# Convolution transforms by sums and differences of mirrored steps, with each block's odd token tiles reversed up to the MLP

## The chip, the core and the metric

The kernel runs on one core of a Trainium2 chip. The metric is the device time of one execution in microseconds, lower is better. The core has a matrix engine (TensorE, PE in the profile; its weight loads are PEld), a vector engine (VectorE, DVE), an activation engine (ScalarE, ACT), a general engine (GpSimd, POOL) and a queue that issues most of the loads (SyncE, SP).

## The reference, cut to what matters

One transformer layer over 8 blocks of 512 tokens by 256 features. The part that the change touches is a causal convolution of each feature along the 512 tokens (steps) of a block, written with Fourier transforms, between two scale-and-shift steps:

```python
x = layernorm(x_text) ; scale_in, shift_in = split(c_t @ W_film_in + b_film_in)
x = x * (1 + gate * scale_in) + gate * shift_in
# s4d: causal convolution along the steps, by Fourier transforms of length 2 L
Kf = rfft(K, n=2 * L); xf = rfft(x, n=2 * L, axis=1)
y  = irfft(xf * Kf, n=2 * L, axis=1)[:, :L] + x * D_skip      # here L = 512 steps
y  = y * (1 + gate * scale_out) + gate * shift_out
xt = x_text + y
h  = gelu(layernorm(xt) @ W1 + b1) @ W2 + b2
xt = layernorm(xt + h)
```

Ahead of it stands an attention of the tokens over 1024 context rows (4 heads, the 32 largest scores of each row are kept), whose result `c_t` makes the scales and shifts. Behind it stands a mixture of experts: a shared expert for every token, and one of 8 routed experts, chosen per token.

## The kernel before, in words

**Tiles.** A block's 512 tokens are four tiles of 128 partitions by 256 features. `xm` (input of the convolution), `xr` (its output and then the running sum), `s.xt` (the normalised input) hold these four tiles side by side. The convolution of 512 steps is done on two halves of 256 steps each (in the kernel `L = T // 2 = 256`), with transforms of length 512 that share tables; the second half also gets the first half's share by a second kernel spectrum. Tile t is (half b, part c) with t = 2 b + c, and a product of 512 columns takes part c of both halves at once.

**Transforms.** `ftab` holds cosine and sine tables for 256 frequencies by 256 steps, in 128x128 pieces. `spectrum(src, f, r, name)` makes frequency group f (128 of them) of part r (real, imaginary) with a product over each of the two step groups c. So `mixed` (one call per block) issues for f and r in 0, 1 two products each, 8 of 128x128 by 512 columns, into PSUM tiles `pxf`. VectorE multiplies them with the kernel's spectrum `kf` (tiles `t2`, `t3`, shown as `t`), GpSimd sums into `yf`. The way back is again 8 products, 4 for each step group c, into `py`; ScalarE copies each to `xr`, then two of the four tiles are multiplied and shifted by `film` (its product is `pfo`; `pfi` is the one ahead of the convolution).

**Around it.** `prepare` loads a block (`xt`, `cx`), normalises, transposes with `ident`, and makes queries and keys; it runs one to two blocks ahead. `attention` makes scores (`pS`), finds the 32 largest (`mn`, `hi`, `top`), and weighs the context rows (`e`, `acc`, `pa`, `pu`). `after_mix` normalises (`hh`), transposes (`transposed`, `hT`), runs the MLP (`pm` into `ga`, `am` into the running accumulators `acc`), adds to `xr`, normalises twice more, and runs router and shared expert (`pg`, `p`, `ae`). `routed` runs blocks of one expert's 128 tokens (`pg`, `pu`, `pyr`). Small constant tables are made in `setup`, beside the attention of block 0; there the spectrum of the convolution's own kernel is made from `ktime` into `pf`, then `kf`.

**Order.** Nothing runs in program order. Every operation is noted with a cost by the class `Plan` (`note`, `time`), and `order` lays them out at build time as a list schedule: on each engine, whenever it is free, the ready operation with the lowest number. Attention and `prepare` have their numbers lowered by 100 (`LEAD_A`, `LEAD_P`), the scores raised by 300 (`LEAD_S`). Buffers of one tag are granted in the order in which the tiles were made. `together` interleaves the notes of three streams: attention of block b, everything behind attention of block b - 1 (`behind`), `prepare` of b + 1. On the chip each engine, and SP, then takes its instructions strictly in the planned order. Since all of them are issued from `o.fn()` in `issue`, nearly every operation bears line 323 in the profile; tiles tell them apart.

**Buffers.** General PSUM tiles (`bank`) share 4 banks, tag "mm"; film products and accumulators (`bank2`) have 2, tag "ac". Weights come in 5 buffers of 128x1024, tag "w" (`wpool`): in setup first the time tables `qq`, then `film_in`, `film_out`, then `w1` and `w2` of block 0.

Of the kernel before, what the change touches and what calls it, by code (L numbers as in the profile page):

```python
# [12 lines left out]
F32 = mybir.dt.float32  # L13
# [5 lines left out]
ALU = mybir.AluOpType  # L19
# [3 lines left out]
P = 128  # L23
# [320 lines left out]
def tile_kernel(ctx: ExitStack, tc: tile.TileContext, a: dict, out: bass.AP):  # L344
# [13 lines left out]

    L = T // 2
# [36 lines left out]
    def bank(name, pool=ps_mm, tag="mm"):  # L396
        return pool.tile([P, 512], F32, tag=tag, name=name)
# [4 lines left out]
    def accs(name):  # L402
# [14 lines left out]
                     base=0, channel_multiplier=-1)  # L417
    plan.noting = True
# [12 lines left out]
    def prepare(b, s):  # L431
# [89 lines left out]

    ftab = const.tile([P, 3, NL, L], F32, name="ftab")

# [34 lines left out]
    def row(v, n):  # L558
        return v.rearrange("(o d) -> o d", o=1).broadcast_to([n, v.shape[0]])
# [21 lines left out]
    def transposed(src, tag, name, g=None, b=None):  # L581

        t_ = pr.tile([P, ND, T], F32, tag=tag, name=name)
        for c in range(ND):
            p_ = bank(f"{name}_p{c}")
            for t in range(NT):
                TE.transpose(p_[:, t * P : (t + 1) * P], src[:, t, c * P : (c + 1) * P], ident)
# [6 lines left out]
    def spectrum(src, f, r, name):  # L594

        p_ = bank(name)
        blocks = src.rearrange("p (b c) d -> p c b d", b=2)
        for c in range(NL):
            TE.matmul(p_, ftab[:, r, c, f * P : (f + 1) * P], blocks[:, c],
                      start=(c == 0), stop=(c == NL - 1))  # L600
        return p_.rearrange("p (b d) -> p b d", b=2)


    def setup():
# [248 lines left out]
        V.memset(cf[0:1, 0:1], 1.0 / NFFT)  # L853
        for f in range(NL):
            for r in range(2):
                p3 = spectrum(ktime, f, r, f"pf{f}_{r}")
# [4 lines left out]
                V.scalar_tensor_tensor(k1, k0, alt, k1, ALU.mult, ALU.add)  # L861
            for k in kf:
                V.tensor_copy(k[:, f, 2, :], k[:, f, 0, :])
# [193 lines left out]
    def mixed(b, s):  # L1057
# [9 lines left out]

        yf = pr.tile([P, NL, 2, 2, D], F32, tag="yf", name=f"yf{b}")
        for f in range(NL):
            re, im = (spectrum(xm, f, r, f"pxf{b}_{f}_{r}") for r in range(2))  # L1070
# [12 lines left out]
            yield  # L1083
        xr = s.xr = pr.tile([P, NT, D], F32, tag="xr", name=f"xr{b}")
        for c in range(NL):
            p_ = bank(f"py{b}_{c}")
            steps = [(f, r) for f in range(NL) for r in range(2)]
            for i, (f, r) in enumerate(steps):
                TE.matmul(p_, ftab[:, 2 * r, f, c * P : (c + 1) * P], yf[:, f, r].rearrange("p b d -> p (b d)"),
                          start=(i == 0), stop=(i == len(steps) - 1))  # L1090
            S.copy(xr.rearrange("p (b c) d -> p c b d", b=2)[:, c], p_.rearrange("p (b d) -> p b d", b=2))
            for t in (c, NL + c):
                p_ = film(1, s, t, f"pfo{b}_{t}")
                V.tensor_mul(xr[:, t, :], xr[:, t, :], p_[:, :D])
                V.tensor_add(xr[:, t, :], xr[:, t, :], p_[:, D:])
                GP.tensor_add(xr[:, t, :], xr[:, t, :], s.xt[:, t, :])
            yield

    def after_mix(b, s, between=()):
# [28 lines left out]
        for i in range(2):  # L1128
            V.tensor_add(xr[:, 2 * i : 2 * i + 2], xr[:, 2 * i : 2 * i + 2], acc[i])
# [288 lines left out]
    with tc.If(rows_ok < P):  # L1418
# [6 lines left out]
        V.tensor_copy(tmask, pt[:, : B * NT])  # L1425
        for t_ in (cum, pdone):
            GP.memset(t_, 0.0)
# [54 lines left out]
```

## Time and profile before

| | |
|---|---|
| median of 3 runs | 1792.97 us (1792.47 to 1794.63) |
| the profiled execution | 1794.11 us |
| its span, first to last instruction | 1792.3 us |
| instructions | 21191 |
| mean granted TensorE clock | 0.874 of full |
| PE / DVE / ACT / POOL busy | 1513.1 / 1302.1 / 1154.6 / 931.5 us |

A group line reads: line of the program, engine, operation, output and inputs by the program's names, shapes, count; then the time in which at least one of the group ran, the mean length of one in ns; then the idle time of its engine just before them and what ended it. A window line has the stretch in us, its length, the busy time of PE, PEld, DVE, ACT and POOL with the count of instructions, the granted clock (1.00 is full), the share of the DMA engines and GB/s. A wait line says which engine and tile waited for what: us in total, number of times, longest. An fp32 matrix product appears as two MATMUL records, a transpose as one. Neighbouring matmuls overlap in the record, so sums go by the busy time and not by count times mean.

### The profile page before, as it was taken

The numbers are of one execution on the slowest core, as the hardware profiler recorded it, in microseconds if no ns is written. First come the engines' busy times: TensorE is split into PE (matmuls) and PEld (weight loads), VectorE is DVE, ScalarE is ACT, GpSimd is POOL, SyncE is SP. The second block draws the span as 40 slices with busy tenths as digits, with TensorE's granted clock in tenths as the row PEclk, the third lists the DMA queues.
The fourth block names the chain that finished last, engine by engine and source line by source line (L and its number), as shares of the span: only waits on it lengthen the run. The fifth ranks groups of instructions, "written<-read, shape, count | busy, mean of one in ns | idle before, by whom it ended". The sixth has DMA issues, their size and how long they took to land. (4 is left out here: it accounts for less than half of the span.)

```text
span 1792.3 us, 21191 instructions
## 1 busy us (share of the span) xinstructions
PE 1513.1 (84%) x6363; PEld 893.1 (50%) x6363; DVE 1302.1 (73%) x3073; ACT 1154.6 (64%) x2008; POOL 931.5 (52%) x1072
## 2 busy tenths in 40 slices
PE   5365577797998798999889999998999989889885
PEld 2143333344543454465436554654465547547685
DVE  6989977885878697977798889697978987222210
ACT  4778844676747774887578877885788678123121
POOL 5578544445363645465555765474557646233122
PEclk8555677786998799998989999998999989989898
DMA  4000110001200120143103330431033205523794
GB/s 118 0 1 24 33 35 18 12 12 47 70 20 12 47 65 18 36 128 96 54 12 109 91 102 12 135 107 58 12 111 107 66 12 162 179 103 86 228 280 117
DMA packets 101289, 131.68 MB, mean 73 GB/s; under 512 B 9687, under 2 KB 73004, under 8 KB 101166
## 3 DMA queue, kind: packets, MB, share of 16 engines
q1 hardware_dynamic: 93102, 121.05, 21.1%
q0 software_dynamic: 7008, 8.42, 2.6%
q8 instruction: 52, 0.85, 0.2%
q10 hardware_dynamic: 1056, 0.79, 0.1%
q14 instruction: 71, 0.58, 0.1%
HBM read 112.22 MB, written 18.78 MB: 73 GB/s over the span
## 5 line engine op out<-in xcount | busy, mean ns | idle before, releaser
L323 PE MATMUL pS<-kT,qT 32*128 32x512 f32 x512 | 285.6, 742 | 71.2 <-DVE mn L323 61.0
L323 POOL TENSOR_TENSOR acc<-acc,e 128x1024 f32<-128x1024 f32 x96 | 229.0, 2385 | 182.3 <-ACT e L323 179.9
L323 DVE MAX8 top<-mn 128x8 f32<-128x256 f32 (+1 forms) x512 | 276.0, 556 | 11.9
L323 ACT COPY sc<-pS 128x512 f32<-128x512 f32 x256 | 145.6, 584 | 167.1 <-PE pS L323 136.9
L323 DVE SCALAR_TENSOR_TENSOR e<-sc,t,e 128x1024 f32<-128x1024 f32 x128 | 180.3, 1421 | 40.6 <-ACT e L323 40.3
L323 DVE TENSOR_TENSOR mn<-sc,pS 128x512 f32<-128x512 f32 x256 | 165.2, 677 | 35.9 <-PE pS L323 19.9
L323 POOL TENSOR_TENSOR mn<-mn 128x256 int32<-128x256 int32 x128 | 102.4, 800 | 164.4 <-DVE hi L323 163.8
L323 PEld LDWEIGHTS pS<-kT,qT 32*128 32x128 f32 x512 | 75.9, 208 | 203.6 <-DVE mn L323 98.9
L323 ACT ACTIVATE e<-sc,sm 128x1024 f32<-128x1024 f32 x128 | 145.1, 1146 | 16.1 <-POOL acc L323 13.2
L323 ACT ACT_TABLE_LOAD x118 | 151.4, 1283 | 4.0 <-issue 2.0
L323 PE MATMUL pm<-hT,w 128*128 128x512 f32 x256 | 137.9, 677 | 13.6 <-ACT hT L323 13.6
L323 ACT ACTIVATE junk<-sc,sm 128x1024 bf16<-128x1024 f32 x128 | 146.1, 1141 | 1.3
L323 PEld LDWEIGHTS pu<-aT,cx 128*96 128x96 f32 x1024 | 122.2, 168 | 28.6 <-issue 24.1
L323 PE MATMUL pu<-aT,cx 128*96 128x128 f32 x1024 | 135.4, 282 | 0.2 <-ACT aT L323 0.2
L323 PE MATMUL am<-w,ga 128*128 128x256 f32 x512 | 129.1, 398 | 6.1 <-ACT ga L323 6.1
L323 PEld LDWEIGHTS am<-w,ga 128*128 128x128 f32 x512 | 96.9, 196 | 51.4 <-issue 27.6
L323 POOL DMA_INDIRECT out_dram<-yb,to x38 | 61.5, 1620 | 96.7 <-DMA out_dram<-yb,to 46.3
L323 ACT ACTIVATE e<-e,sm 128x1024 f32<-128x1024 f32 x96 | 108.5, 1147 | 1.6 <-DVE sm L323 1.6
L323 POOL TENSOR_TENSOR mn<-mn,hi 128x256 int32<-128x256 int32 x128 | 104.9, 819 | 8.0
L323 DVE TENSOR_TENSOR ger<-sgr,pu 128x512 f32<-128x512 f32 x38 | 26.0, 684 | 108.7 <-PE pu L323 105.9
L323 DVE MATCH_REPLACE8 mn<-top,mn 128x256 f32<-128x256 f32 x256 | 104.6, 409 | 0.0
L323 POOL TENSOR_TENSOR yf<-yf,t 128x512 f32<-128x512 f32 (+1 forms) x80 | 85.2, 1089 | 35.0 <-DVE t L323 33.7
(287 smaller groups left out, 3125.0 us busy)
## 6 DMA issues: line engine op xcount, KB each, us to landing
rt_gate<-in_L_ffn_rt_gate_dram SPq DMA_DIRECT2D x38, 512.0 KB
rt_up<-in_L_ffn_rt_up_dram SPq DMA_DIRECT2D x38, 512.0 KB
rt_down<-in_L_ffn_rt_down_dram SPq DMA_DIRECT2D x38, 512.0 KB
w<-in_L_xattn_W_dram SPq DMA_DIRECT2D x32, 512.0 KB
cx<-in_ctx_dram SPq DMA_DIRECT2D x7, 768.0 KB
xtab<-zt SPq DMA_DIRECT2D x8, 642.5 KB
xb<-xtab SPq DMA_DIRECT2D x38, 128.5 KB
xt<-in_x_dram SPq DMA_DIRECT2D x8, 512.0 KB
```

What stands on the lines that cost most here:

```text
L323: o.fn()
```

## The change

The second part of each half (odd tiles t = 1 and 3, 128 steps) is kept in reverse order of its tokens from `prepare` to the MLP. Step p of an even tile then lies on the same partition as its mirror step L - 1 - p in the odd tile. A cosine or sine table at half-step offset is even or odd under this mirroring, depending on the parity of the frequency. So the frequencies are grouped by parity instead of by halves of the range, and each group's real and imaginary part needs only the sum or only the difference of the two tiles: one product of 128 steps instead of two. Backwards, the four spectra give two results, `pyu` and `pyw`, with two products each, whose sum and difference are the even and odd tiles.

- `prepare` transposes the odd tiles with `anti` (ones on the counter-diagonal) in place of `ident`, then reverses the odd tiles of `s.xt` and of its scale `rs2` by products with `anti` (`pr`) and copies on ScalarE.
- `mixed` makes `df` and the sum in place of `xs` on VectorE, four products, four backwards, one copy, a subtraction and an addition on VectorE; then film for the four tiles.
- `after_mix` transposes `hh`'s odd tiles with `anti`, which puts the MLP's input back in token order. `xr`'s odd tiles are added to the MLP's accumulators by a product with `anti`, and copied out by ScalarE; the even tiles are added by VectorE as before.
- `setup` loads the tables as `ktab` and `htab` (in the "w" buffers) and sorts them into `ftab` and `itab` by three copies on ScalarE. The spectrum of the kernel itself is still made with two products each, with columns picked by parity; `spectrum` is gone.
- The general pass (`attention_masked`, only where a check at the end fails) gets its token mask reversed.

```diff
+    anti = const.tile([P, P], F32, name="anti")
+    GP.memset(anti, 0.0)
+    GP.affine_select(anti, anti, pattern=[[1, P]], compare_op=ALU.not_equal, fill=1.0,
+                     base=-(P - 1), channel_multiplier=1)
+    turn = (ident, anti)
...
-                TE.transpose(p_[:, t * P : (t + 1) * P], s.xt[:, t, c * P : (c + 1) * P], ident)
+                TE.transpose(p_[:, t * P : (t + 1) * P], s.xt[:, t, c * P : (c + 1) * P], turn[t % 2])
             S.copy(xT[:, c, :], p_)
         yield
+        for v, n in ((s.xt, D), (s.rs2.unsqueeze(2), 1)):
+            p_ = bank(f"pr{b}_{n}")[:, : 2 * n].rearrange("p (b d) -> p b d", b=2)
+            x1 = v.rearrange("p (b c) d -> p c b d", c=2)[:, 1]
+            TE.matmul(p_, anti, x1, start=True, stop=True)
+            S.copy(x1, p_)
...
-    ftab = const.tile([P, 3, NL, L], F32, name="ftab")
+    ftab = const.tile([P, 2, 2, P], F32, name="ftab")
+    itab = const.tile([P, 2, 2, P], F32, name="itab")
...
-        for i, r in enumerate((0, 1, 1)):
-            SY.dma_start(ftab[:, i], ft[:, 0, r, :NL, :L])
+        ktab = wpool.tile([P, 1024], F32, tag="w", name="ktab").rearrange("p (r c f) -> p r c f", r=2, c=NL)
+        htab = wpool.tile([P, 1024], F32, tag="w", name="htab")[:, : 2 * L].rearrange("p (r f) -> p r f", r=2)
+        for r in range(2):
+            SY.dma_start(ktab[:, r], ft[:, 0, r, :NL, :L])
+            SY.dma_start(htab[:, r], ft[:, 1, r, 0, :L])
+        S.copy(ftab, htab.rearrange("p r (j g) -> p r g j", g=2))
+        S.copy(itab[:, 0], ktab[:, :, 0].rearrange("p r (n two) -> p two r n", two=2)[:, 1])
+        S.copy(itab[:, 1], htab.rearrange("p r (n two) -> p two r n", two=2)[:, 1])
+        SY.dma_start(ftab[:, 1, 0, 0:1], altc)
+        SY.dma_start(itab[0:1, 0, 1, :], altr)
         for c in range(NL):
-            SY.dma_start(ftab[:, 1, c, 0:1], altc)
-            SY.dma_start(ftab[0:1, 2, 0, c * P : (c + 1) * P], altr)
+            SY.dma_start(ktab[:, 1, c, 0:1], altc)
...
+        xs, xd = (xm.rearrange("p (b c) d -> p c b d", c=2)[:, k] for k in range(2))
+        df = pk.tile([P, 2, D], F32, tag="sg", name=f"df{b}")
+        V.tensor_sub(df, xs, xd)
+        V.tensor_add(xs, xs, xd)
...
-            re, im = (spectrum(xm, f, r, f"pxf{b}_{f}_{r}") for r in range(2))
+            re, im = bank(f"pxf{b}_{f}_0"), bank(f"pxf{b}_{f}_1")
+            for r, p_ in enumerate((re, im)):
+                TE.matmul(p_, ftab[:, r, f], xs if f == r else df, start=True, stop=True)
...
-        for c in range(NL):
-            p_ = bank(f"py{b}_{c}")
-            steps = [(f, r) for f in range(NL) for r in range(2)]
-            for i, (f, r) in enumerate(steps):
-                TE.matmul(p_, ftab[:, 2 * r, f, c * P : (c + 1) * P], yf[:, f, r].rearrange("p b d -> p (b d)"),
-                          start=(i == 0), stop=(i == len(steps) - 1))
-            S.copy(xr.rearrange("p (b c) d -> p c b d", b=2)[:, c], p_.rearrange("p (b d) -> p b d", b=2))
-            for t in (c, NL + c):
...
+        pu, pw = bank(f"pyu{b}"), bank(f"pyw{b}")
+        for p_, k in ((pu, 0), (pw, 1)):
+            for f in range(NL):
+                r = f if k == 0 else 1 - f
+                TE.matmul(p_, itab[:, f, r], yf[:, f, r].rearrange("p b d -> p (b d)"),
+                          start=(f == 0), stop=(f == NL - 1))
+        x0, x1 = (xr.rearrange("p (b c) d -> p c b d", c=2)[:, k] for k in range(2))
+        pw3 = pw.rearrange("p (b d) -> p b d", b=2)
+        S.copy(x0, pu.rearrange("p (b d) -> p b d", b=2))
+        V.tensor_sub(x1, x0, pw3)
+        V.tensor_add(x0, x0, pw3)
+        for t in range(NT):
...
-        hT = transposed(hh, "hT", f"hT{b}", gff, bff)
+        hT = transposed(hh, "hT", f"hT{b}", gff, bff, turn)
...
+            if k == 0:
+                for t in range(1, NT, 2):
+                    TE.matmul(acc[t // 2][:, 1, :], anti, xr[:, t, :], start=False, stop=False,
+                              skip_group_check=True)
...
-            V.tensor_add(xr[:, 2 * i : 2 * i + 2], xr[:, 2 * i : 2 * i + 2], acc[i])
+            V.tensor_add(xr[:, 2 * i], xr[:, 2 * i], acc[i][:, 0])
+            S.copy(xr[:, 2 * i + 1], acc[i][:, 1])
```

More of the change, by code (lines that the diff above doesn't have):

```diff
@@ L579, in normalise, with transposed @@
                          scale=rs[:, t : t + 1])
-    def transposed(src, tag, name, g=None, b=None):
+    def transposed(src, tag, name, g=None, b=None, turn=(ident, ident)):
         t_ = pr.tile([P, ND, T], F32, tag=tag, name=name)
@@ L586, in transposed @@
             for t in range(NT):
-                TE.transpose(p_[:, t * P : (t + 1) * P], src[:, t, c * P : (c + 1) * P], ident)
+                TE.transpose(p_[:, t * P : (t + 1) * P], src[:, t, c * P : (c + 1) * P], turn[t % 2])
             if g is None:
@@ L592, in transposed @@
         return t_
-    def spectrum(src, f, r, name):
-        p_ = bank(name)
-        blocks = src.rearrange("p (b c) d -> p c b d", b=2)
-        for c in range(NL):
-            TE.matmul(p_, ftab[:, r, c, f * P : (f + 1) * P], blocks[:, c],
-                      start=(c == 0), stop=(c == NL - 1))
-        return p_.rearrange("p (b d) -> p b d", b=2)
     def setup():
@@ L853, in setup @@
         V.memset(cf[0:1, 0:1], 1.0 / NFFT)
+        ktab_ = ktab.rearrange("p r c (j g) -> p r c g j", g=2)
+        lags = ktime.rearrange("p (b c) d -> p c b d", b=2)
         for f in range(NL):
             for r in range(2):
-                p3 = spectrum(ktime, f, r, f"pf{f}_{r}")
+                p_ = bank(f"pf{f}_{r}")
+                for c in range(NL):
+                    TE.matmul(p_, ktab_[:, r, c, f], lags[:, c], start=(c == 0), stop=(c == NL - 1))
+                p3 = p_.rearrange("p (b d) -> p b d", b=2)
                 c_ = cf[:, f : f + 1]
@@ L860, in setup @@
                 V.tensor_scalar(k1, p3[:, 1], c_, None, ALU.mult)
-                V.scalar_tensor_tensor(k1, k0, alt, k1, ALU.mult, ALU.add)
+                V.tensor_tensor(k1, k1, k0, ALU.subtract if f else ALU.add)
             for k in kf:
@@ L1065, in mixed @@
             yield
+        xs, xd = (xm.rearrange("p (b c) d -> p c b d", c=2)[:, k] for k in range(2))
+        df = pk.tile([P, 2, D], F32, tag="sg", name=f"df{b}")
+        V.tensor_sub(df, xs, xd)
+        V.tensor_add(xs, xs, xd)
         yf = pr.tile([P, NL, 2, 2, D], F32, tag="yf", name=f"yf{b}")
         for f in range(NL):
-            re, im = (spectrum(xm, f, r, f"pxf{b}_{f}_{r}") for r in range(2))
+            re, im = bank(f"pxf{b}_{f}_0"), bank(f"pxf{b}_{f}_1")
+            for r, p_ in enumerate((re, im)):
+                TE.matmul(p_, ftab[:, r, f], xs if f == r else df, start=True, stop=True)
+            re, im = (p_.rearrange("p (b d) -> p b d", b=2) for p_ in (re, im))
             y = yf[:, f]
@@ L1084, in mixed @@
         xr = s.xr = pr.tile([P, NT, D], F32, tag="xr", name=f"xr{b}")
-        for c in range(NL):
-            p_ = bank(f"py{b}_{c}")
-            steps = [(f, r) for f in range(NL) for r in range(2)]
-            for i, (f, r) in enumerate(steps):
-                TE.matmul(p_, ftab[:, 2 * r, f, c * P : (c + 1) * P], yf[:, f, r].rearrange("p b d -> p (b d)"),
-                          start=(i == 0), stop=(i == len(steps) - 1))
-            S.copy(xr.rearrange("p (b c) d -> p c b d", b=2)[:, c], p_.rearrange("p (b d) -> p b d", b=2))
-            for t in (c, NL + c):
[L1093 to L1097, printed above, removed]
+        pu, pw = bank(f"pyu{b}"), bank(f"pyw{b}")
[10 more added lines that the diff above has]
+        for t in range(NT):
+            p_ = film(1, s, t, f"pfo{b}_{t}")
+            V.tensor_mul(xr[:, t, :], xr[:, t, :], p_[:, :D])
+            V.tensor_add(xr[:, t, :], xr[:, t, :], p_[:, D:])
+            GP.tensor_add(xr[:, t, :], xr[:, t, :], s.xt[:, t, :])
+            if t % 2:
+                yield
     def after_mix(b, s, between=()):
@@ L1425, in tile_kernel @@
         V.tensor_copy(tmask, pt[:, : B * NT])
+        pt = bank("pt_an")
+        TE.matmul(pt[:, : B * NT], anti, tmask, start=True, stop=True)
+        odd = slice(1, B * NT, 2)
+        V.tensor_copy(tmask[:, odd], pt[:, odd])
         for t_ in (cum, pdone):
```

## The prediction

> **What bounds the kernel now.** I read four views in this order: the page's busy shares and slices, one window over the steady stretch, the waits of TensorE in it, and four windows around the convolution.
>
> ```profile
> PE 1513.1 (84%) x6363; PEld 893.1 (50%) x6363; DVE 1302.1 (73%) x3073; ACT 1154.6 (64%) x2008; POOL 931.5 (52%) x1072
> PE   5365577797998798999889999998999989889885
> ...
> DVE  6989977885878697977798889697978987222210
> ...
> PEclk8555677786998799998989999998999989989898
> ```
>
> Three stages show. Up to about 315 us (seven slices) VectorE is nearly full, TensorE half busy at half clock: setup beside block 0's attention. From about 630 to 1530 us TensorE stands at 8 to 9: one block's attention beside the convolution, MLP and experts of the block before. Behind 1530 us the last block runs with VectorE almost empty. The time is mostly made in the middle one:
>
> ```profile
> 630.00:1530.00 900.00, 841.71 (x3440) 491.32 (x3439) 746.32 (x1836) 681.18 (x1174) 519.93 (x624) 0.95 0.25 75
> ```
>
> The columns are length, then PE, PEld, DVE, ACT, POOL busy. TensorE is busy 841.7 of 900 us, VectorE 746.3: 94% against 83%. What TensorE waits for in that window:
>
> ```profile
> PE pc L323 <- DMA cx<-in_ctx_dram: 15.8, 3, 6.0
> PE pyr L323 <- DVE ger L323: 11.0, 7, 3.1
> PE hT_p L323 <- ACT hh L323: 10.2, 5, 3.8
> PE pm L323 <- ACT hT L323: 7.9, 5, 4.6
> PE pS L323 <- ACT sc L323: 4.6, 4, 2.3
> PE pS L323 <- DVE mn L323: 3.8, 6, 1.2
> ```
>
> Its scores (`pS`) wait 3.8 us for VectorE in 900. So in this stage VectorE does not hold TensorE up; TensorE is the nearer bound, with a load (`cx`) and the normalisation chain behind the convolution (`hh`, `hT`) as the gaps. The same around the forward transform of four blocks:
>
> ```profile
> 870.00:890.00 20.00, 20.00 (x57) 8.64 (x55) 18.04 (x34) 10.96 (x20) 13.21 (x9) 1.00 0.00 0
> 1050.00:1070.00 20.00, 20.00 (x55) 8.39 (x54) 16.56 (x32) 14.28 (x22) 15.19 (x13) 1.00 0.26 73
> 1230.00:1260.00 30.00, 30.00 (x74) 12.78 (x73) 22.30 (x47) 15.58 (x29) 14.10 (x13) 0.85 0.00 0
> 1410.00:1440.00 30.00, 29.43 (x87) 13.39 (x87) 28.28 (x63) 15.42 (x26) 20.50 (x21) 1.00 0.00 1
> ```
>
> TensorE is full (99.4 of 100 us), but VectorE has 85.2: little room for what the change puts there.
>
> **The change part by part.** Rows by shape that price it:
>
> ```profile
> L323 PE MATMUL py<-yf,ftab 128*128 128x512 f32 x128 | 58.8, 600 | 0.7 <-POOL yf L323 0.7
> L323 PE MATMUL pxf<-xm,ftab 128*128 128x512 f32 x128 | 58.8, 600 | 0.0
> L323 DVE TENSOR_TENSOR t<-pxf,kf 128x512 f32<-128x512 f32 x32 | 21.2, 680 | 1.4 <-POOL yf L323 1.4
> L323 DVE TENSOR_TENSOR ta<-ta,tk 128x512 f32<-128x512 f32 x8 | 12.9, 1616 | 0.2
> L323 DVE TENSOR_TENSOR tk<-tk,ta 128x512 f32<-128x512 f32 x8 | 9.0, 1126 | 6.2 <-POOL ta L323 6.0
> L323 PE MATMUL am<-w,ga 128*128 128x256 f32 x512 | 129.1, 398 | 6.1 <-ACT ga L323 6.1
> ```
>
> An fp32 product is two records, so 8 products each of `pxf` and `py` per block are 64 products a group, and 58.8/64 = 0.92 us each. By the busy time, not by the mean of 600 ns, since neighbours overlap.
>
> Forward transform: 8 products become 4: -3.67 us of TensorE. Before them VectorE makes a difference and a sum (`df`, `xs`) of 128x512, both inputs in SBUF: 2 x 1.13 to 2 x 1.62 us. [...] They stand between `xm` and the first product, and need all four tiles of it where the first two sufficed before.
>
> Inverse: 8 products become 4: -3.67 us. ScalarE copies once instead of twice (-0.58, `xr<-py` 583 ns), VectorE subtracts and adds from PSUM: 2 x 0.68 = 1.36 us. All four tiles wait for them; before, two tiles went ahead. Both `pyu` and `pyw` hold a PSUM bank for these 1.36 us longer. Other users of these four banks pay at most that in turn; I take nothing, as the removed products free the same banks earlier.
>
> Reversal of odd tiles in `prepare`: transposes with `anti` cost what those with `ident` cost. Added are one product of 512 columns (0.92), one of 2 columns (at most the 0.31 of a `pg<-gate,hdT` product, 19.9/64), and two ScalarE copies (0.585 and about 0.2, as `sm<-t` of 128x2). TensorE +1.2, ScalarE +0.8 us. It runs a block ahead of its reader, so the copies are hidden behind attention; TensorE's 1.2 is not where it is full. Without the cover ScalarE's copies cost 0.8 us a block.
>
> MLP: two products of 256 columns (129.1/256 = 0.50 each): +1.0 us. VectorE adds 2 x 128x256 (0.42) instead of 2 x 128x512 (0.68), -0.5; ScalarE copies the other two tiles, +0.73 (`xbT<-pxb`, 365 ns).
>
> Per block: TensorE -7.35 + 1.2 + 1.0 = -5.1; VectorE 2.7 + 1.36 - 0.5 = +3.6; ScalarE -0.58 + 0.8 + 0.73 = +0.95; GpSimd nothing. Over eight blocks -41, +28, +8 us.
>
> Setup: three table loads of 256 KB become two of 256 and two of 128 KB, four one-element-column loads remain four. So SP issues 8 where it issued 7. The old loads were issued at 17 to 24 us into own memory; `ktab` and `htab` take two of the five `w` buffers and can only load when the time table's `qq` lets go, where SP now issues the first `w1` (191 us) and three more `w` (213 to 226 us). These `w` move two places back; their first reader is at 363 us, so over 100 us cover it, and without the cover it would be two loads of some 4 us. `ktab`'s reader `pf` starts at 238.7 us; between lie the landing, an ACT copy (`itab`), and the small `alt` loads behind that copy on SP. SP's queue there holds the parameter loads that the setup's end waits for. I take +1 us, from 0 to +6 if SP or ScalarE stand in line. Three ScalarE copies (0.6 + 2 x 0.4) are in it, and a memset and a select on GpSimd at the start (0.2 + 0.28 us by `ident`'s) lie before its 6.7 us wait.
>
> Last block (behind 1540 us): attention is gone, the chain is bare. `xm` is complete at 1567.8, `pxf` starts at 1568.4, GpSimd's first sums at 1572.2, the second end at 1583.4, `py` ends at 1586.4. New: sums of 2 x 1.13, then two products instead of four: GpSimd starts about 0.7 later; behind its end 2 products instead of 4 are left (-1.8), then subtract and add (+1.36) and two more tiles of film on VectorE (+1.7). With +1.0 and -0.5 of the MLP I come to about +1 us, from -2 to +3. The expert loads behind 1676 us are not touched.
>
> Blocks 0 to 6, two views. By the whole block of 180 us: TensorE 169 -> 163.9 at the same 93.9% is -5.5 us; VectorE then has 153.8 of 174.5, 88%. By the stage alone: the four windows' VectorE work of 85.2 plus 4 x 4.1 = 101.6 us at 97%, the most it reaches for long, is 104.7 us against 100: +1.2 each, with 1.2 for the reversal in full windows and 0.7 of the MLP +3.1. The truth depends on whether attention's VectorE work is displaced into the later windows of the block, where VectorE has some 10 us free. The missing wait of `pS` for VectorE speaks for the first view; I take -2.5 of the span -5.5 to +3.1.
>
> [...] The row: granted clock 0.59 at 920 to 930 us, where TensorE waited for `hh` and `hT`, and 0.50 through most of the setup. [...] Removed products lengthen such gaps. [...]
>
> Sum: 7 x -2.5 + 1 + 1 = -15.5 us. The profiled execution took 1794.1 us (span 1792.3), 1.1 above the median of 1793.0; so 1793 - 15 = 1778.
>
> **The rivals.**
>
> 1. VectorE becomes the bound of the convolution's stage: 7 x 3.1 + 2 = +24, or about 1812 with some of attention displaced (+19). For it: VectorE at 9.5 to 9.9 us in 10 through much of 880 to 930, 1250 to 1300 and 1400 to 1460 us. Against: 83% over the block. It decides once VectorE has over 97% of the stretch from `pfi` to `pm` while TensorE waits for `df`, `xs` or `hh`.
>
> 2. Everything is gained: -5.1 to -5.5 in each of seven blocks, 1757. Against: the gaps at `cx` (33.8 us in the whole trace) and `hh` are not TensorE's work and remain.
>
> 3. The gain turns into the wait for `cx`. The load of the block after next is issued when the last `pu` of a block has read the buffer, and TensorE stands in order before it, 5 to 6 us at 860 and 1222 us. The order is written by the planner from its costs, so changed costs move such waits; one more or less in each of three blocks is 16 us either way, and with the gain eaten it is no change, 1793.
>
> 4. The whole is not what it says: a failed check at the end would run the general pass over all blocks. The counts it tests don't depend on token order; under 1%.
>
> **How the numbers follow.** The forecast (own range 1766 to 1788) 0.45; rival 1 0.36; rival 2 0.05; rival 3 0.13, of which no change 0.07, slower 0.04 and faster 0.02; rival 4 0.01. Faster 0.52, within 0.2% (3.6 us, about what a measurement can tell apart) 0.07, slower 0.41. The range goes from full gain with one wait less in hand, 1755, to rival 1 without displacement, 1817.
>
> **What would show it.** Right: `pxf` and `py` groups at half their count and about 29 us each; TensorE's busy sum near 1470; blocks of 177 to 178 us between forward transforms; `df` and `xs` of 1.1 to 1.6 us. Wrong: TensorE below 92% in 630 to 1530 us with waits for `df`, `xs`, `x1` or a longer one for `hh`; granted clock lower behind the convolution; `ktab` copies with ScalarE idle before them; more than 15.8 us of wait for `cx`.

## The result, and the profile after

| | before | after |
|---|---|---|
| median of 4 runs each | 1793.72 us (1792.47 to 1794.63) | 1864.76 us (1860.91 to 1867.97) |
| ratio | 1 | 1.0399, 95% interval 1.0373 to 1.0425 |
| the profiled execution | 1794.11 us | 1867.88 us |
| its span | 1792.3 us | 1866.2 us |
| mean granted TensorE clock | 0.874 | 0.846 |

The change makes the kernel 71 us slower. The forecast was 15 us faster; its range ended at 1817 us.

The page of the changed kernel, its busy sums and slices:

```profile
PE 1520.6 (81%) x6299; PEld 897.3 (48%) x6299; DVE 1319.7 (71%) x3105; ACT 1165.2 (62%) x2038; POOL 943.0 (51%) x1074
...
PE   6356667797889697998789988998899979879896
...
PEclk8556567696888698999989987999899889879898
```

There are 64 TensorE instructions fewer, yet TensorE is busy for longer (1513.1 before). The reason is in the clock row: 6, 7 and 8 stand where before had 9. In the trace of before, 128x512 fp32 records that follow each other without a gap start every 429 ns at granted clock 1.00 and every 854 ns at 0.50, so the same product takes twice as long there, and busy time is no measure of work when the clock changes. The steady stretch, cut to match the 630 to 1530 us of before, and what TensorE waited for in it:

```profile
652.00:1598.00 946.00, 847.68 (x3395) 495.04 (x3394) 749.24 (x1826) 675.75 (x1172) 518.87 (x617) 0.91 0.24 71
```

```profile
PE hT_p L323 <- ACT hh L323: 29.5, 5, 6.7
PE pc L323 <- DMA cx<-in_ctx_dram: 18.3, 4, 5.1
PE pS L323 <- ACT sc L323: 8.9, 13, 2.0
PE pfo L323 <- DVE xr L323: 4.4, 2, 3.0
PE pyu L323 <- POOL yf L323: 4.4, 1, 4.4
PE pyw L323 <- POOL yf L323: 3.9, 3, 1.6
```

The stretch is 46 us longer. TensorE's share falls from 94% to 90%, the granted clock from 0.95 to 0.91, and VectorE is busy for about the same time (746.3 before). The wait for `hh` has tripled (10.2 before), the one for `sc` doubled (4.6), and the inverse transform and the film product behind it wait for `yf` and `xr`, which they hardly did. Two waits shrank: `pyr` for `ger` (11.0 to 3.6) and `pm` for `hT` (7.9 to 2.6). The groups that the change made:

```profile
L323 PE MATMUL pyw<-yf,itab 128*128 128x512 f32 x32 | 20.7, 741 | 8.8 <-POOL yf L323 7.9 <-DVE t L323 0.8
L323 PE MATMUL pyu<-yf,itab 128*128 128x512 f32 x32 | 19.9, 708 | 12.1 <-POOL yf L323 12.0
L323 PE MATMUL pxf<-xm,ftab 128*128 128x512 f32 x32 | 17.4, 631 | 0.0
L323 PE MATMUL pxf<-df,ftab 128*128 128x512 f32 x32 | 17.1, 626 | 0.0
L323 DVE TENSOR_TENSOR xm<-xm 128x512 f32<-128x512 f32 x8 | 7.6, 948 | 0.3
L323 DVE TENSOR_TENSOR df<-xm 128x512 f32<-128x512 f32 x8 | 6.8, 848 | 0.3
```

The counts are halved as planned. But the two backward groups cost 40.6 us together instead of 29.4, because their records have a mean of 741 and 708 ns where before had 600: 16 of the 64 ran in whole or in part at clock 0.50, and the waits ahead of them are for GpSimd's `yf`.

**A table for all runs.** From each trace I take TensorE's busy time in the span and, from the clock record, how much of it was at clock 0.5. Half of that is lost: "lost to half clock". Busy time less this loss is the work at full clock, and span less busy time is idle. The clock record begins 13 to 33 us into the span; ahead of it the products have the lengths of half clock (in the changed kernel 1061 ns for a 128x512 record, against 592 at full clock), so TensorE's 5 to 20 us there are counted as half clock. All in us. The three parts add up to the span of the profiled execution, not to the median; ratios are to before's runs on the same chip.

| run | median | ratio (95%) | work at full clock | lost to half clock | idle |
|---|---|---|---|---|---|
| before | 1793.7 | | 1364 | 149 | 279 |
| after | 1864.8 | 1.0399 (1.0373 to 1.0425) | 1320 | 201 | 346 |
| x1_reversal | 1830.2 | 1.0211 (1.0173 to 1.0249) | 1379 | 166 | 280 |
| x2_transforms | 1867.5 | 1.0417 (1.0376 to 1.0459) | 1323 | 189 | 352 |
| x3_twice | 1871.2 | 1.0424 (1.0381 to 1.0467) | 1367 | 188 | 318 |
| x4_half | 1845.8 | 1.0298 (1.0260 to 1.0335) | 1311 | 202 | 327 |
| x5_same_order | 1807.0 | 1.0081 (1.0061 to 1.0101) | 1309 | 185 | 311 |
| x6_sums | 1834.2 | 1.0218 (1.0148 to 1.0289) | 1307 | 220 | 311 |
| x7_sums_both | 1831.1 | 1.0210 (1.0137 to 1.0282) | 1311 | 191 | 321 |
| x8_filler | 1792.9 | 1.0003 (0.9987 to 1.0019) | 1364 | 150 | 276 |
| x9_after_filler | 1892.0 | 1.0534 (1.0509 to 1.0559) | 1374 | 190 | 332 |
| x10_less_vector | 1796.6 | 1.0008 (0.9992 to 1.0024) | 1363 | 150 | 282 |
| x11_both_less | 1801.1 | 1.0026 (1.0010 to 1.0041) | 1311 | 182 | 309 |
| x12_filler_less | 1795.8 | 1.0005 (0.9990 to 1.0021) | 1363 | 153 | 278 |
| before, factor 1.04 | 1839.1 | 1.0269 (1.0246 to 1.0291) | 1370 | 173 | 293 |
| before, factor 1.06 | 1818.1 | 1.0147 (1.0127 to 1.0166) | 1365 | 147 | 297 |
| before, factor 1.10 | 1856.6 | 1.0335 (1.0311 to 1.0359) | 1369 | 189 | 307 |
| after, factor 1.00 | 1896.4 | 1.0566 (1.0518 to 1.0613) | 1330 | 210 | 357 |
| after, factor 1.06 | 1860.8 | 1.0389 (1.0366 to 1.0411) | 1330 | 179 | 345 |
| after, factor 1.10 | 1836.2 | 1.0237 (1.0205 to 1.0269) | 1312 | 180 | 340 |

In the changed kernel TensorE has 44 us less to do, loses 52 us more to the half clock and is idle for 66 us more: -44 + 52 + 66 = +74, as in the span. The work was saved as forecast. More than it came back, as idle time and as half clock.

### The profile page after: what moved, and what is told of

It reads as the page before. It is cut to its first block, busy times and chain, and to the rows that moved or that the text cites. A ratio compares the mean times of both kernels' runs of the same rounds, so it can differ in the third digit from the quotient of the medians.

```text
span 1866.2 us, 21121 instructions
## 1 busy us (share of the span) xinstructions
PE 1520.6 (81%) x6299; PEld 897.3 (48%) x6299; DVE 1319.7 (71%) x3105; ACT 1165.2 (62%) x2038; POOL 943.0 (51%) x1074
## 5 line engine op out<-in xcount | busy, mean ns | idle before, releaser
L323 DVE SCALAR_TENSOR_TENSOR e<-sc,t,e 128x1024 f32<-128x1024 f32 x128 | 187.2, 1475 | 23.1 <-ACT e L323 22.1
L323 POOL TENSOR_TENSOR yf<-yf,t 128x512 f32<-128x512 f32 (+1 forms) x80 | 90.5, 1177 | 84.4 <-DVE t L323 83.3
```

## The experiments

The theories on record were these. A: the removed products turn into idle TensorE, and the half clock behind it takes the rest. B: the reversal costs. C: the planner makes a new order from any changed cost, and an order is worth tens of us. D: VectorE's added sums displace attention.

**The change in parts.** `x1_reversal` is before with the reversal alone:

```diff
+    turn = (ident, anti)                      # and in prepare, transposed, after_mix as in the change
```

> The kernel before with the reversal alone: odd tiles reversed in prepare by two products and two copies, transposes with anti, the product with anti in the MLP, the copies of the odd tiles there; the transforms are the old ones, so the convolution works on reversed odd tiles and its values are not the reference's. Added by the sum of the prediction: TensorE 2.2 us, ScalarE 1.5 us, VectorE -0.5 us a block. Theory A (the removed products turn into idle TensorE and half clock behind it): +5 to +18 us, as TensorE is still full. Theory B (the reversal is what costs, by its place in prepare and its PSUM banks): +45 us or more. Theory C (the planner's order is a draw of a lottery, any change moves it by tens of us): anything from -20 to +70. Theory D (VectorE's new sums displace attention): +5 to +18 us.

`x2_transforms` is the changed kernel without the reversal:

```diff
-    turn = (ident, anti)
+    turn = (ident, ident)                     # and no pr, no product of xr with anti
```

> The changed kernel without the reversal: no products with anti, transposes with ident, the MLP's sum on VectorE as before; the new transforms then work on tiles in token order and the values are not the reference's. TensorE -7.35, VectorE +4.1, ScalarE -0.6 us a block against before. Theory A: +35 to +60 us against before, most of the loss. Theory B: -20 to +10. Theory C: anything. Theory D: +35 to +60.

`x3_twice` issues each transform product of the changed kernel twice:

```diff
-                TE.matmul(p_, ftab[:, r, f], xs if f == r else df, start=True, stop=True)
+                for _ in range(2):
+                    TE.matmul(p_, ftab[:, r, f], xs if f == r else df, start=True, stop=True)
...
-            for f in range(NL):
+            for f in [*range(NL)] * 2:
```

> The changed kernel with each product of the two transforms issued twice into the same place, so TensorE's saving of 7.35 us a block is taken back and all else stays. If TensorE bounds the stage, +45 to +58 us on the changed kernel's 1865. Theory A: within 15 us of the changed kernel, or faster than it, with TensorE's idle time in the convolution's stage down by some 50 us and less half clock behind it. Theory B: +20 to +58. Theory D: +20 to +58, as the added products come on top of VectorE's delay. Theory C: anything.

`x4_half` is before with half the products of the transforms left out and nothing put in:

```diff
-        for c in range(NL):
+        for c in range(nl):                   # nl = 1 for the blocks' spectra
...
-            steps = [(f, r) for f in range(NL) for r in range(2)]
+            steps = [(f, r) for f in range(NL) for r in range(2) if r == (f if c == 0 else 1 - f)]
```

> The kernel before with half of the products of both transforms left out (one step group of two forward, two spectra of four backward), nothing added; its values are not the reference's. TensorE -7.35 us a block. If TensorE bounds the stage: -35 to -55 us against before. Theory A: between -10 and +20 us, as the stage's length is that of its chain over VectorE, GpSimd and ScalarE, and the products' time turns into idle time. Theory B and D: -25 to -55. Theory C: anything.

Measured: 1830.2, 1867.5, 1871.2 and 1845.8 us. The parts don't add up: +37 and +74 against +71 for both. Twice the products cost 6 us, and leaving work out of before, with nothing added, makes it 3% slower. So the time doesn't follow TensorE's work. B alone falls, since the kernel without the reversal is as slow as with it, and D alone falls, since `x4_half` is slower with no sums in it. But each of these kernels also has an order of its own, since the planner plans from the costs it sees. The next runs separate work from order.

**Work in a fixed order.** In `x5_same_order` the products left out are still noted, with their cost, but their function does nothing when issued:

```diff
+                plan.ghost = r != (f if c == 0 else 1 - f)
...
-                    plan.note(name, method, partial(f, *args, **kw), args, kw)
+                    fn = partial(f, *args, **kw) if not plan.ghost else int
+                    plan.note(name, method, fn, args, kw)
```

> The kernel before with every instruction of every engine kept in its place, but half the products of the sequence blocks' two transforms not issued: of each forward spectrum one product of two, of each inverse bank two of four, so the convolution is incomplete. The planner still charges for the products left out, so the order it writes is that of before. It is the run x4_half (1845.8 us) with before's order in place of the order that the planner makes when it knows of the shorter work. Theory A, the saved time turns into idle TensorE and half clock whatever the order: 1793 to 1850, that is no gain, and near x4_half if the loss is in the work itself. Theory C, the loss is in the order that the planner writes: faster than before, by some part of 8 blocks x about 8 products x 0.6 us = 38 us: 1755 to 1788, and 58 to 90 us under x4_half.

Measured 1807.0 us. That answers for A: with every other instruction in its place, taking 55 us of work from TensorE (1364 to 1309) makes the kernel 14 us slower. And it is 39 us faster than `x4_half`, which does the same work in its own order. For a stretch by stretch view I cut blocks 0 to 6 from the first `pxf` to the first `hT_p`, the conv stage. First block 4's row and the sum of the seven for before, then the same two rows for `x5_same_order`:

```profile
1055.65:1093.57 37.92, 36.58 (x125) 17.48 (x124) 32.26 (x76) 23.16 (x41) 25.84 (x27) 1.00 0.06 18
...
sum 286.54, PE 263.53 PEld 120.44 DVE 258.42 ACT 159.45 POOL 194.27; mean PE 37.65 PEld 17.21 DVE 36.92 ACT 22.78 POOL 27.75
```

```profile
1059.08:1102.48 43.40, 39.76 (x109) 17.94 (x108) 32.70 (x78) 23.58 (x42) 26.18 (x28) 0.76 0.04 14
...
sum 301.24, PE 253.15 PEld 112.90 DVE 260.10 ACT 159.61 POOL 194.90; mean PE 36.16 PEld 16.13 DVE 37.16 ACT 22.80 POOL 27.84
```

The seven stages take 14.7 us more; the MLP's stages (from the first `hT_p` to the first `hdT_p`) and the experts' (from there to the next block's first `pxf`) are within 1 us of before (526.4 and 458.3 against 526.3 and 457.3). By the clock record these 14.7 are: work at full clock 255 to 208 (-47), lost to half clock 8 to 45 (+36), idle 23 to 48 (+25). Block 4 shows how. TensorE's waits in its stage, then the stage in steps of 4 us (columns: length, busy PE, PEld, DVE, ACT, POOL, then the granted clock):

```profile
PE pS L325 <- DVE mn L325: 1.9, 1, 1.9
PE pS L325 <- ACT sc L325: 1.1, 1, 1.1
PE py L325 <- POOL yf L325: 0.6, 1, 0.6
```

```profile
1058.00:1062.00 4.00, 3.06 (x8) 1.07 (x6) 3.54 (x9) 2.80 (x5) 2.24 (x4) 1.00 0.35 112
1062.00:1066.00 4.00, 3.79 (x12) 1.77 (x13) 4.00 (x6) 2.29 (x5) 1.42 (x2) 0.81 0.00 0
1066.00:1070.00 4.00, 4.00 (x5) 1.20 (x5) 0.91 (x4) 2.37 (x3) 3.70 (x4) 0.50 0.00 0
1070.00:1074.00 4.00, 4.00 (x9) 1.75 (x8) 3.91 (x7) 2.49 (x3) 2.79 (x2) 0.84 0.00 0
1074.00:1078.00 4.00, 4.00 (x22) 2.45 (x20) 3.79 (x14) 2.31 (x5) 3.92 (x4) 1.00 0.00 0
1078.00:1082.00 4.00, 3.10 (x7) 1.06 (x6) 4.00 (x7) 2.42 (x7) 0.80 (x2) 1.00 0.00 0
1082.00:1086.00 4.00, 2.40 (x4) 0.59 (x4) 3.90 (x11) 3.88 (x6) 1.55 (x1) 0.87 0.00 0
1086.00:1090.00 4.00, 4.00 (x5) 1.00 (x4) 2.77 (x7) 0.59 (x1) 4.00 (x4) 0.50 0.00 0
1090.00:1094.00 4.00, 4.00 (x7) 1.34 (x7) 0.00 (x0) 1.47 (x4) 1.16 (x2) 0.50 0.02 4
1094.00:1098.00 4.00, 4.00 (x13) 2.62 (x12) 2.53 (x9) 2.58 (x5) 1.52 (x3) 0.50 0.00 0
```

TensorE, without the removed products, arrives early: at 1061 us ScalarE's copy `sc` is not done, at 1078 `yf` is not, at 1082 VectorE's `mn` is not. Each gap is small, 3.6 us in all. But behind the first the clock is 0.50 for 6.8 us and behind the other two for 13.7, TensorE is 4.00 of 4.00 busy in the slow slices, and now it is TensorE that is late: VectorE has nothing at all to do from 1090 to 1094. In before the same stage ran at 1.00 throughout, with 1.3 us of idle TensorE, nearly all of it at the end. The removed products had been covering the waits.

**What the removed products were worth as cover.** `x8_filler` has the products of `x5_same_order` and, ahead of each, one on constants, which needs no `xm` and no `yf`; their number is that of before again (the forward half is shown):

```diff
+        def filler(p_, f, r):
+            TE.matmul(p_, ident, ftab[:, 0].rearrange("p c f -> p (c f)"), start=True, stop=True)
...
-            re, im = (spectrum(xm, f, r, f"pxf{b}_{f}_{r}") for r in range(2))
+            re, im = (spectrum(xm, f, r, f"pxf{b}_{f}_{r}", filler, product) for r in range(2))
```

> x5_same_order with each product that it leaves out replaced by one on constants (the identity and a table), issued ahead of the real product into the same bank, so that TensorE has it to do while the real one still waits for xm or yf. It is before's count of products and before's order, but only half of them carry data. If x5_same_order lost its saved 47 us to the half clock (44.7 us lost in the conv stages of blocks 0 to 6, before 8.4): the clock stays up, 1783 to 1797. If it lost them to the waits alone, the fillers change nothing: 1803 to 1811. Output incomplete as in x5_same_order.

Measured 1792.9 us, before's time, with the loss to half clock back at 150. Its conv stages, then the group of its backward products that carry data, then that group in `x5_same_order`:

```profile
sum 286.51, PE 263.72 PEld 120.40 DVE 258.39 ACT 159.39 POOL 194.16; mean PE 37.67 PEld 17.20 DVE 36.91 ACT 22.77 POOL 27.74
```

```profile
L69 PE MATMUL py<-yf,ftab 128*128 128x512 f32 x64 | 31.2, 602 | 0.2 <-POOL yf L330 0.2
```

```profile
L325 PE MATMUL py<-yf,ftab 128*128 128x512 f32 x64 | 41.6, 774 | 18.3 <-POOL yf L325 18.3
```

The same 64 records wait 0.2 instead of 18.3 us and take 602 instead of 774 ns when products whose results nobody reads stand in front of them. So in before's order half of the transforms' products cost no time, and as cover for the waits of the other half they were worth 14 us.

**VectorE's sums.** `x6_sums` adds the change's `df` and `xs` to `x5_same_order`, unseen by the planner; `x7_sums_both` also puts the inverse's two in place of ScalarE's second copy:

```diff
+            if t == NT - 1:
+                plan.then(lambda: V.tensor_sub(df, xs, xd), lambda: V.tensor_add(xs, xs, xd))
...
+            if c:                                          # x7_sums_both
+                plan.instead(lambda: (V.tensor_sub(x1, df, pw3), V.tensor_add(df, df, pw3)))
```

> x5_same_order (before's order on every engine, half the transform products, 1807.0 us) with the change's two forward sums put in on VectorE: after the last write of xm, df = difference and xs = sum, 2 x 512 columns, and the products read them. The planner doesn't know of the two sums, so all else keeps before's order. The inverse's sums are left out, so the output is incomplete. If VectorE sets the end of the convolution (it is busy 259.0 of the 286.5 us of the conv stages of blocks 0 to 6 in before), the sums come on top: 8 x (1.2 + 1.4) = +21: 1822 to 1832. If they lie beside other work: 1803 to 1812.

> x6_sums with the inverse's two sums on VectorE as well, reading the second bank py, in place of ScalarE's second copy of the bank. With this the loop's work is that of the changed kernel without the reversal, in before's order (the sums' results are not carried through, the output is incomplete). If VectorE sets the end: another 8 x 1.4 = +11 over x6_sums: 1833 to 1845, which would leave 20 to 30 of the changed kernel's 1864.8 for its order. If not: 1803 to 1815, and the other 50 to 60 us are the order that the planner makes.

Measured 1834.2 and 1831.1 us. The forward sums cost 27 us, with wide runs (1822.9 to 1849.1): by the interval of the ratio 14 to 39 us over `x5_same_order`. The inverse's cost nothing that can be seen in VectorE's time; but in `x7_sums_both` the even tiles don't wait for them, as they do in the changed kernel, so what that wait costs was not measured. The forward ones, 1.5 us per block, stand where everything behind them waits. Two waits of `x6_sums`:

```profile
PE pxf L69 <- DVE xm L69: 13.7, 7, 3.5
PE py L330 <- POOL yf L330: 11.9, 6, 2.8
```

The first is new: TensorE stands before `pxf` in seven of the eight blocks, 2 us each. The clock follows again: 220 us lost to it, the most of all runs.

So with the changed kernel's products and sums in before's order the time is 1831, +37 (1.0210, interval 1.0137 to 1.0282). Another 34 are missing to 1865.

**The order alone.** In the six draws that follow no instruction of the loop is changed, only one factor by which the planner scales its costs of TensorE's work (of no other engine's, other than the first expectation has it):

```diff
-SLOW = 1.05
+SLOW = 1.06        # p1_before_106, p2_after_106; 1.04: p3_before_104; 1.10: p_b_slow110, p_a_slow110; 1.00: p_a_slow100
```

> The kernel before with the planner's factor on the costs of TensorE's and the other engines' work (SLOW) at 1.06 in place of 1.05: not one instruction is added or removed, only their order can differ. Theory A: the order does not matter much, 1783 to 1803. Theory C: another draw of an order, between 1800 and 1860, since before's factor gave a good one; such a number would put the 71 us that the change cost inside what a change of order alone can do.

> The kernel before with the factor at 1.04. Theory A: 1783 to 1803. Theory C: 1800 to 1860, and not the same as at 1.06.

> The kernel before with the planner's factor at 1.10. Draws of before so far: 1793.7 at 1.05, 1818.1 at 1.06, 1839.1 at 1.04. If before's own order is an unusually good one: 1805 to 1850. If not: below 1800.

> The changed kernel with the same factor at 1.06 in place of 1.05, nothing else. Theory A: within 10 us of the changed kernel, 1855 to 1875. Theory C: a new order, anywhere from 1790 to 1870, and more likely lower than 1865 than higher.

> The changed kernel with the planner's factor at 1.10. If the changed kernel's time is before's 1793, plus 38 for its work in a fixed order, plus a draw of the order that costs 25 to 45: 1845 to 1885. If its order is unusually bad: below 1840.

> The changed kernel with the factor at 1.00. As for 1.10: 1845 to 1885 if its order is an ordinary draw, below 1840 if it is an unusually bad one.

Measured for before 1818.1, 1839.1 and 1856.6 us, for after 1860.8, 1836.2 and 1896.4. A factor that adds and removes no instruction of the loop costs before between 24 and 63 us, so theory C holds too: before's order, at the factor it came with, is the best of its four, 33 us under their mean, and each of the three changes of cost gave it up. The changed kernel's order at 1.05 is the third of its four, at their mean. Its draw at 1.10 is below 1840, which the expectation took as a sign that the one at 1.05 is unusually bad; the draw at 1.00 is far above and says the opposite. The means of four orders each, 1827 for before and 1865 for after, differ by 38 us: the same as `x7_sums_both` found in one fixed order. With orders that scatter by 60 us this agreement is partly luck: before's slowest order is slower than the changed kernel's fastest, and four draws of each leave the 38 uncertain by about as much as itself. The fixed order is the firmer of the two.

**Where the changed kernel itself loses.** What does not overlap is TensorE's idle time: 279 to 307 us in before's four orders, 340 to 357 in the changed kernel's. By stages, the two kernels at factor 1.05 (all in us, before and after):

| stage | length | idle | lost to half clock |
|---|---|---|---|
| ahead of the first `pxf` | 298, 304 | 128, 125 | 65, 67 |
| seven conv stages | 287, 273 | 23, 78 | 8, 18 |
| seven MLP stages | 526, 565 | 56, 56 | 33, 53 |
| seven experts' stages | 457, 494 | 34, 40 | 36, 51 |
| from the last `pxf` | 224, 230 | 39, 46 | 7, 11 |

```profile
sum 272.76, PE 194.28 PEld 89.35 DVE 235.90 ACT 126.75 POOL 179.23; mean PE 27.75 PEld 12.76 DVE 33.70 ACT 18.11 POOL 25.60
```

That is the sum of the conv stages after. They are 14 us shorter than before's, although TensorE stands idle in them for 55 us more: its work there falls by 79 us at full clock, more than the 47 that leaving out the products took from them in `x5_same_order`, and 33 us of work more stands in the MLP's and experts' stages (the reversal's products, by the forecast 2.2 us a block, would be about 15 us of this). Those two lose the time: 33 us in this work and 36 in the clock. The largest new wait is at the end of the conv stage, in the whole trace of before and then of after:

```profile
PE hT_p L323 <- ACT hh L323: 19.0, 7, 5.1
PE hT_p L323 <- ACT hh L323: 44.4, 8, 6.7
```

It is 16 to 25 us in before's four orders and 17 to 20 with the products left out or the sums put in, in before's order. It is 42 to 46 us in all four of the changed kernel's, and 42 in `x4_half`. So the removed products do turn into idle time in the changed kernel too, but in the planner's own orders mostly at another place than in before's; what in these orders makes that wait was not tested.

**Fillers in the changed kernel.** `x9_after_filler` issues a product on constants ahead of each transform product of the changed kernel, in its own order:

```diff
+                plan.first(lambda p_=p_: filler(p_))
```

> The changed kernel, whole and in its own order on every engine, with one product on constants issued ahead of each transform product of the loop (8 per block, 64 in all, 0.6 us each at full clock), which the planner doesn't know of. If the half clock behind the idle stretches of the conv stage is a cause of the slowdown: 1840 to 1858. If not, unchanged or longer by what fillers delay: 1862 to 1880. x3_twice had the same number of products but its own order, 1871.2.

Measured 1892.0 us, 27 slower than the changed kernel: a miss. In the changed kernel's order the conv stages lose only 18 us to the half clock, and the fillers put 46 us of full-clock work there for 10 of the 78 us of idle time. Half of that idle time, 39 us, is the wait of `hT_p` for `hh`, behind the last product of the transforms, where no filler stands; with the fillers it is still 38. The fillers of `x8_filler` stood in the gaps (18.3 us of waits for `yf` became 0.2); these mostly didn't.

**What sets the length of the conv stage.** After `x5_same_order` I thought it was VectorE, as it is busy for 258 of 286.5 us. `x10_less_vector` leaves out two of VectorE's four multiplications per half, in before's order, `x11_both_less` does it on top of `x5_same_order`, `x12_filler_less` on top of `x8_filler`:

```diff
             V.tensor_mul(t3[:, 0], bc(re[:, 0], 1, 2), kf[1][:, f, 0:2])
+            plan.instead(int)
...
             GP.tensor_add(y[:, :, 1], y[:, :, 1], t3[:, 0])
+            plan.instead(lambda y=y, t2=t2: GP.tensor_add(y[:, :, 1], y[:, :, 1], t2[:, 0]))
```

> The kernel before, in its own order on every engine and with all its products, with two of VectorE's four multiplications per half of the spectrum left out (those that make t3, 680 ns each by the trace of before; 4 per block, 32 in all, 21.8 us), and GpSimd reading t2 where it read t3; so the convolution is incomplete. If VectorE sets the length of the conv stage: faster by nearly all of it, 1772 to 1782. If TensorE does, as the forecast had it: 1789 to 1797.

> x5_same_order (half the transform products) and x10_less_vector (two of VectorE's four multiplications per half left out) in one, in before's order; incomplete as both are. If the two engines set the length together: the conv stages of blocks 0 to 6 shrink from 286.5 to about 260 to 275, in all 1765 to 1783. If the half clock takes whatever TensorE is spared, or GpSimd's part sets the length: 1795 to 1810, as x5_same_order.

> x8_filler (half the products carry data, the other half are on constants and wait for nothing) with x10_less_vector's two multiplications left out, in before's order. If TensorE's own issue is what is left once VectorE is relieved: as before, 1789 to 1797. If the waits of the data-carrying products for VectorE and GpSimd are: 1772 to 1785.

Measured 1796.6, 1801.1 and 1795.8 us. All three say that my second theory was wrong as well. The sums of the conv stages of `x10_less_vector` and `x11_both_less`:

```profile
sum 287.91, PE 265.34 PEld 120.47 DVE 241.61 ACT 159.31 POOL 194.16; mean PE 37.91 PEld 17.21 DVE 34.52 ACT 22.76 POOL 27.74
```

```profile
sum 291.38, PE 244.63 PEld 108.22 DVE 243.57 ACT 159.28 POOL 195.94; mean PE 34.95 PEld 15.46 DVE 34.80 ACT 22.75 POOL 27.99
```

VectorE relieved of 17 us in these stages: no gain, TensorE is full. TensorE relieved: no gain, in `x5_same_order` it stands idle for 48 us of these stages and loses 45 to the half clock. Both relieved: 6 us faster than `x5_same_order` (its conv stages are 10 us shorter), so VectorE counts for something once TensorE has gaps, but still 291 us, with 47 us idle and 35 lost to the half clock, and the largest wait is for GpSimd's `yf` (18.5 us), whose five sums per half nobody shortened. Without that half clock these stages would be at most 35 us shorter, by this trace's own numbers; no run here has both engines relieved and the clock up, since the fillers of `x12_filler_less` fill TensorE again. So what sets the stage when all three engines and the order are free to change stays open. No version ran measurably faster than before.

## Why the prediction was wrong, point by point

- **The work.** Right: -41 us on TensorE was forecast, 44 were measured at full clock (1364 to 1320). The sign for it, "TensorE's busy sum near 1470", was badly chosen, since busy time grows when the clock falls: it rose to 1520.6. VectorE was to have +28, its busy sum rose by 17.6.
- **"TensorE is the nearer bound."** This is the step that failed first: that taking 5.1 us of TensorE's work from a block would take 2.5 us from its time. `x5_same_order` took 55 us of it in all and was 14 us slower. The bound was read from 94% against 83% and from waits of `pS` for VectorE of 3.8 us in 900. A row of 20.00 busy in 20.00 says that TensorE had no gap, not that its end sets anything: `x8_filler` has the same full rows with half of the products on constants, and the same time. "The missing wait of `pS` for VectorE speaks for the first view" was the same error. The wait was missing because TensorE was kept busy just long enough; take the products away and it appears (`pS` for `mn` and `sc`, `py` for `yf`).
- **"I take -2.5 of the span -5.5 to +3.1."** In before's order the halved products were worth +1.8 us per block (14/8) and the forward sums another +3.3 (27/8). Even the upper end was too low.
- **The clock.** The forecast's sum has no term for it; the changed kernel loses 52 us more to the half clock than before does. In before's order new gaps opened inside the conv stage, and the loss there rose from 8 to 45 us in seven blocks (`x5_same_order`). "Removed products lengthen such gaps" was right for the changed kernel, whose wait of `hT_p` for `hh` grew from 19.0 to 44.4 us, but the clock's loss in its conv stages rose by 10 us only; 20 and 15 more were lost in the MLP's and experts' stages, which the forecast left out. Gaps shorter than 3.41 us, the shortest span in the clock record, were followed by falls: 1.15 us in block 4 of `x5_same_order`, in a window that also held eight transposes and a score product.
- **"The order is written by the planner … 16 us either way."** It saw the mechanism and missed the size. Neutral changes cost before 24, 45 and 63 us, always upwards, because before's order was a good one. This is large enough for the other half of the 71 us.
- **Rival 1**, VectorE as the bound at 1812, had the right sign and a right place, the sums ahead of `pxf`; that they cost 27 us, near its 24 for the whole change, is luck. But `x10_less_vector` shows that VectorE is not the bound in its sense: added work there costs, removed work gains nothing.
- **The sums.** No run shows the 2.7 us a block that the forecast put in for the two forward sums, and that its +3.6 of VectorE and the 3.1 of its span hold; it was the author's estimate, between the rows of `tk` and `ta`. The trace has 948 and 848 ns, 1.8 us a block: the twelve sums with GpSimd idle throughout took 691 to 693 ns, the four with GpSimd busy for 44 to 97% of their time 691, 980, 1651 and 2736 ns. The rows of `ta` and `tk`, same shape and inputs, were poor neighbours (1616 and 1126 ns): of their 16 records the four with GpSimd idle throughout took 672 to 693 ns, and the eleven with GpSimd busy for over 60% of their time 878 to 2736 ns, so both rows are means over records of both kinds. GpSimd's busy sum, for which nothing was forecast, rose by 11.5 us; with the sums in before's order it did not (928.9 in `x7_sums_both` against 931.5), so the sums as such don't explain it.
- **Setup and last block.** +1 was forecast for each, with 0 to 6 and -2 to +3 as bounds; the first `pxf` starts 6 us later (303.8 against 298.2), at the bound, and the stretch behind the last one is 6 us longer (230.2 against 224.0), outside it.
- **The reversal.** Priced at 2.2 us per block on TensorE and 1.5 on ScalarE. `x1_reversal` is 37 us slower than before, but in an order of its own, within the range of the neutral draws; its cost in a fixed order was not measured. `x2_transforms`, without it, is as slow as the changed kernel.

The account: 14 for the halved products, 24 to 27 for the forward sums, together 37 to 40 in before's order; the other 34 lie within what a new order costs before by itself. That the order makes all of these 34, and the reversal and the wait for the inverse's sums none, is an inference from the spread, not a measurement. In its own order the changed kernel also loses its time at other places than in before's.

## What to carry to other kernels

A full engine is not yet the engine that sets the time. Before taking work from it, ask who it will wait for once it is early, and try it with the order held fixed: leave the instruction in the plan and don't issue it. Look at the granted clock behind small gaps, which can cost more than their length (3.6 us of gaps and 10.2 us lost to the half clock behind them in block 4 of `x5_same_order`); a product that covers a wait may be worth keeping (14 us here, by `x8_filler`). Where a list scheduler writes the order, measure a change against several orders of each version, not against one that happens to be good.

## What the runs showed of the hardware

- In the clock records of before and after the granted clock is 1.00 or 0.50, and its spans, but for the last, which the record's end cuts, are multiples of 3.41 us; in block 4 of `x5_same_order` they are 6.83 and 13.65. Most falls came without an idle stretch of 3.41 us: of 25 falls in before behind 315 us, 23 had at least 1.1 us of idle TensorE in the 3.4 us ahead of them, and only 4 had 3.3 or more. But 15 of 22 windows with 0.9 to 1.8 us of idle time passed without a fall. All windows of 3.41 us at full clock in before behind 315 us, cut on the record's grid:

| idle TensorE in the window | windows | clock fell at the end |
|---|---|---|
| under 0.9 us | 327 | 2 |
| 0.9 to 1.8 us | 22 | 7 |
| 1.8 us or more | 17 | 16 |

- All nine falls with less than 1.8 us of idle time had score products `pS` (`32*128` in the profile's rows) or transposes `hT_p` in the window; of the 15 windows with 0.9 to 1.8 us that kept the clock, three had such products. In `x5_same_order` all seven falls of this kind had `pS` or transposes too. No run varies such products alone.
- In block 4 of `x5_same_order` 3.6 us of gaps were followed by 20.5 us at half clock, which is 10.2 us lost, nearly three times their length.
- Products on constants in front of waiting ones shortened one kernel: 64 of them took `x5_same_order` from 1807.0 to 1792.9 us (`x8_filler`). In the changed kernel, where they closed little of the idle time (10 of 78 us in the conv stages), they cost: 64 of them, 54 us of work at full clock, took the changed kernel from 1864.8 to 1892.0 us (`x9_after_filler`).
